# Moving statistics, bias adds and operand sums in the order of a fused decoder kernel

## The chip, the cores and the metric

The kernel runs on one core of one Trainium2 chip. The metric is the device time of one execution, in microseconds (us). All data are 32-bit floats. TensorE (PE) does the matmuls and transposes, VectorE (DVE), ScalarE (ACT) and GpSimd (POOL) the rest, and SyncE (SP) issues the DMAs.

## The reference

One pre-norm decoder layer on x of 4 sequences x 2048 positions x 512 features, in three residual parts:

```python
x = x + _L0_attn_ref(_layernorm(x), ...)    # a linear recurrence over the first axis (4 steps), in 8 blocks of 64
x = x + _L0_xattn_ref(_layernorm(x), ctx)   # cross-attention to 77 keys, 16 heads of 32
x = x + _L0_ffn_ref(_layernorm(x), ...)     # 512 -> 2048, butterfly, gelu, butterfly, 2048 -> 512
```

The layer norm subtracts the mean and divides by the root of variance + 1e-5; it has no weights. In the last part the butterflies (11 stages of 2x2 mixing) are linear, so `up butterfly` and `down butterfly` can be multiplied into the two weight matrices. Biases stand before the gelu (`hbias` in the kernel) and at the output (`b_con + down_bias`, `ybias` in the kernel).

## The kernel before, in words

**Units.** The 2048 positions are cut into 16 units of 128 positions, each with all 4 sequences: a tile `xt` of 128 x 4 x 512, which is updated in place. The work of a unit has two halves: `front` (first and second residual part, and the third norm) and `feed_forward` (third part). While `feed_forward(u)` runs, it draws the steps of `front(u+1)`, a Python generator, in between its own matmuls.

**Slots and steps.** `feed_forward` calls `step()` after every two matmul calls; one such piece is a slot. A matmul call of these shapes is two instructions on TensorE, so a slot is four. Of 108 slots (7 x 8 in the first product, then 26 x 2 in the second), the first 98 are used to draw 54 steps of the front (L762): step n is drawn at slot 98n/54, rounded up; in the first unit the first 8 slots (`lead`) are left out.

**A front,** in the order of its steps: `normed_pairs` (first norm: statistics, rows `xp`, transposes L599), four steps of the recurrence (`ps_s`, L629), `normed` (second norm: statistics, rows `xn` L561, transposes L570, copies `xnt` by ScalarE), `seven` (the query product in seven block products by Strassen's scheme, `ps_q`), attention for four t (scores `ps_sc`, exponentials by ScalarE into `pr` L679, transposes `ps_pt`, `ps_o`), the operand sums `sw` (L713 to L716), `seven` again (`ps_w`, L614, added onto `xt` in L722 and L726), and `normed` again (third norm). `combine` (L741 to L744) then makes the operand sums for the first product of the feed-forward.

**The statistics** (`norm_stats`): four L535 on VectorE, each 128 x 512, four L536, and a chain of 13 small steps on 128 x 4 elements (L541 to L548; an inverse square root by Newton's method). `normed` yields a number of steps between the statistics and the rows (2 in the second norm, 3 in the third).

**feed_forward.** The first product takes p = 0 to 7, seven block products each (L776): `up_head` (3), `up_tail` of the one before (2), `up_mid` (2), with adds on VectorE (L795, L807, L808, L816, L819) and gelu on ScalarE (L781). At each p a slice of `xt` gets the output bias on GpSimd (L844; in the first unit two larger adds, L847). The second product (L872) is made of 26 block products (`DOWN`); its left operands are sums that GpSimd makes (`made`, L829) and its right operands come from DRAM (`dn26`, L865). Results are added onto `xt` (L887, L889).

**The right operands.** The 26 right operands are 8 plain quarters of rows of the second weight matrix and 18 sums of them, in two rings of nine (`RIGHT`). `_right_sums` makes the 18 sums for one of four quarters j, `_right_stores` stores the two rings and the plain part to `dn26` (three DMAs, L151). Quarter 0 is made in the preparation, wholly on GpSimd (L140); quarters 1 to 3 are made during p = 0, 1, 2 of the first unit's feed-forward, 11 of the 18 sums on GpSimd (the names in `SLOW`) and 7 on VectorE (L142). A ring can be written again when its store has landed. The rows of quarters 1 to 3 in SBUF are later used for other things: for weights and activations (`w2` holds the weights for p = 4).

**The preparation** (`_prepare`) multiplies the butterflies into the weights. It has its own generator, and the loop at L971 draws one step of it (n = 0 to 40) and mostly one of `front(0)`.

**What sets the order.** The program is traced in Python order, and a planner then orders the instructions of each engine by their place in the program and by when it expects their inputs. In the preparation the orders of TensorE, SyncE and GpSimd are fixed by hand (L925), and for p < 4 of the first unit that of TensorE. Elsewhere an instruction may be moved ahead of others that were traced before it. `tc.keep_in_program_order(i)` pins instruction `i` behind the instruction of its engine that was traced just before it. In the kernel before it is used for the first statistics of unit 1 alone:

```python
yield from normed_pairs(xt, got, tc.keep_in_program_order if u == 1 else lambda i: i)
```

Of the kernel before, what the change touches and what calls it, by code (L numbers as in the profile page):

```python
# [14 lines left out]
ALU = mybir.AluOpType  # L15
AX = mybir.AxisListType

P = 128
T, B, D = 4, 2048, 512
# [5 lines left out]
NU = B // P  # L25
# [53 lines left out]
          ("20", "b21", "+", "b31"), ("17", "9", "+", "b31"), ("10", "14", "+", "20"), ("19", "b30", "-", "17"),  # L79
          ("22", "b01", "+", "15")))  # L80
PLAIN = tuple(f"b{k}{n}" for k in range(4) for n in range(2))
SLOW = "12", "9", "7", "18", "15", "16", "20", "17", "10", "19", "22"
SLOT = {name: i for i, name in enumerate([row[0] for lot in RIGHT for row in lot] + list(PLAIN))}
SLOT.update({str(i): SLOT[b] for i, b in ((11, "b01"), (13, "b10"), (23, "b11"), (25, "b20"), (3, "b30"), (6, "b30"),
                                          (0, "b31"), (21, "b31"))})
# [45 lines left out]
def _right_sums(nc, j, wdn, rings, alone):  # L131

    made = {f"b{k}{d}": wdn[:, 4 * j + k, d * (D // 2) : (d + 1) * (D // 2)] for k in range(4) for d in range(2)}
    for lot, ring in zip(RIGHT, rings):
        w = ring.rearrange("p (s d) -> p s d", s=len(lot))
        for i, (name, x, op, y) in enumerate(lot):
            made[name] = w[:, i, :]
            x, y, op = made[x], made[y], ALU.add if op == "+" else ALU.subtract
            if alone or name in SLOW:
                nc.gpsimd.tensor_tensor(made[name], x, y, op)  # L140
            else:
                nc.vector.tensor_tensor(made[name], x, y, op)  # L142


def _right_stores(nc, j, wdn, rings, dn26):
    lots = [ring.rearrange("p (s d) -> p s d", d=D // 2) for ring in rings]
    lots.append(wdn[:, 4 * j : 4 * j + 4, :].rearrange("p k (n d) -> p (k n) d", n=2))
    at = 0
    for w in lots:
        n = w.shape[1]  # L150
        nc.sync.dma_start(out=dn26[at : at + n, :, j, :].rearrange("s p d -> p s d"), in_=w)  # L151
        at += n


# [346 lines left out]
def kernel(ctx: ExitStack, tc: tile.TileContext, x, ctx_t, ssm_vec, ssm_vt, ssm_vinv, wq_t, wk_t, wv_t,  # L501
                        wo_t, wexp_t, up_low, up_high, up_bias, dn_low, dn_high, wcon, b_con, down_bias, out):
    nc = tc.nc
# [13 lines left out]
    ybias = const.tile([P, D], F32, name="ybias")  # L517
# [53 lines left out]
            nc.scalar.copy(xnt[:, :, t, :], ps)  # L571
        res.append(xnt)

    def normed_pairs(xt, res, keep):


        mv, y = norm_stats(xt, keep)
        xpt = work.tile([P, T // 2, D // NS, P], F32, tag="xnt", bufs=2, name="xpt")
        half = D // 2
        yield  # L580
        rows = {}

        def row(n):
            i, h = divmod(n, 2)
            rows[n] = work.tile([P, NC, 2, NS], F32, tag="xn", name="xp")
            for k in range(2):
                t = 2 * i + k
                nc.vector.tensor_scalar(rows[n][:, :, k, :], xt[:, t, h * half : (h + 1) * half].rearrange("p (f n) -> p f n", n=NS),
                                        mv[:, t, 0:1], y[:, t : t + 1], ALU.subtract, ALU.mult)

        row(0)
        for n in range(T):
            i, h = divmod(n, 2)
            if n + 1 < T:
                row(n + 1)
            yield
            ps = psum.tile([P, NC, P], F32, tag="f", name="ps_t")
            for f in range(NC):
                nc.tensor.transpose(ps[:, f, :], rows[n][:, f, :, :].rearrange("p k n -> p (k n)"), ident)  # L599
            nc.scalar.copy(xpt[:, i, NC * h : NC * h + NC, :], ps)  # L600
        res.append(xpt)
# [17 lines left out]
    def front(u, xt, res, wq=None):  # L619


        got = []
        yield from normed_pairs(xt, got, tc.keep_in_program_order if u == 1 else lambda i: i)
        xpt = got.pop()
        for c in range(NC):
            ps = psum.tile([P, T, P], F32, tag="f", name="ps_s")
# [89 lines left out]
        nc.gpsimd.tensor_tensor(s4, a12, s2, ALU.subtract)  # L716
        yield
        yield
        left = {1: a11, 2: a12, 3: s4, 4: a22, 5: s1, 6: s2, 7: s3}

        def onto(r):
# [6 lines left out]
        yield from seven((1, 6, 2, 7, 5, 4, 3), lambda i, r, k: left[i][:, k, r, :], lambda i, r, k: wo[:, i - 1, k, :], "w",  # L728
                         {1: spread, 6: onto(r12), 2: onto(r11), 7: onto(r22), 5: onto(r22), 4: onto(r21), 3: onto(r12)})

        yield from normed(xt, got, 3)
        res.append((u, xt, got.pop()))
        if u:
            combine(res[-1][2], res)

    def combine(xnt, res):

# [9 lines left out]
    def feed_forward(u, xt, rhs, other):  # L747
# [9 lines left out]
        lead = 0 if u else 8  # L757

        def step():
            slot[0] += 1  # L760
            past = slot[0] - lead
            for _ in range(max(past, 0) * 54 // (98 - lead) - max(past - 1, 0) * 54 // (98 - lead)):  # L762
                next(other, None)

        def bank(tag):
# [65 lines left out]
        for p in range(h):  # L831
            with tc.manual_schedule(engines={mybir.EngineType.PE}) if u == 0 and p < 4 else nullcontext():
                up_head(p)
                if p:
                    up_tail(p - 1)
                up_mid(p)
            if u == 0 and p < 3:
                _right_sums(nc, p + 1, wdn, rings, False)
                _right_stores(nc, p + 1, wdn, rings, dn26)
            if p == (1 if u else 6) and u + 2 < NU:  # L840
                xts[u + 2] = load_x(u + 2)
            r, d = xt[:, p // 2, p % 2 * (D // 2) : (p % 2 + 1) * (D // 2)], slice(p % 2 * (D // 2), (p % 2 + 1) * (D // 2))
            if u:
                nc.gpsimd.tensor_tensor(r, r, ybias[:, d], ALU.add)  # L844
            elif p % 2 and p > h // 2:
                r = xt[:, p - 5 : p - 3, :]
                nc.gpsimd.tensor_tensor(r, r, ybias.unsqueeze(1).to_broadcast([P, 2, D]), ALU.add)  # L847
            if p >= h // 2:
                made(*plan.pop(0)[1:])
        up_tail(h - 1)  # L850
# [6 lines left out]
        for kind, where, *rest in plan:  # L857
# [3 lines left out]
            i, name, goes = DOWN[rest[0]]  # L861
            n = rest[0] % 2
# [14 lines left out]
            while goes:  # L877
# [5 lines left out]
                d = int(to[0][2]) * (D // 2)  # L883
                r = xt[:, t : t + (k - 1) * by + 1 : by, d : d + D // 2]
# [27 lines left out]
    at, homes = 0, {}  # L912
# [5 lines left out]
    spare = {n: homes[n].rearrange("p (j q) -> p j q", q=P) for n in own}  # L918
    spare.update({n: tb[:, i].rearrange("p (j q) -> p j q", q=P) for i, n in enumerate(lent)})
    rings = [arena[:, i * 9 * D // 2 : (i + 1) * 9 * D // 2] for i in range(2)]  # L920
    xts = {}
    ready = []
    early = []
    E = mybir.EngineType
    with ExitStack() as stack, tc.manual_schedule(engines={E.PE, E.SP, E.Pool}):  # L925
# [45 lines left out]
        for n, _ in enumerate(prep):  # L971
            if n == 27:
                _right_sums(nc, 0, wdn, rings, True)
            if n not in (10, 24, 25, 26):
                next(first, None)
            if n == 3:
                quarter_loads(wo, wo_t, (0, 1, 2, 6))
                nc.gpsimd.tensor_tensor(wo[:, 4], wo[:, 6], wo[:, 0], ALU.subtract)
                nc.gpsimd.tensor_tensor(wo[:, 6], wo[:, 2], wo[:, 6], ALU.subtract)
                nc.gpsimd.tensor_tensor(wo[:, 5], wo[:, 2], wo[:, 4], ALU.subtract)  # L980
                nc.gpsimd.tensor_tensor(wo[:, 3], wo[:, 1], wo[:, 5], ALU.subtract)
            if n == 24:
                xts[1] = load_x(1)
            if n == 25:
                early.append(work.tile([P, 7, 2, P], F32, tag="qt", bufs=1, name="w_second"))
                nc.sync.dma_start(out=early[1], in_=up7[1])
            if n == 17:
                early.append(work.tile([P, 7, 2, P], F32, tag="pt", bufs=1, name="w_first"))
                nc.sync.dma_start(out=early[0], in_=up7[0])
# [19 lines left out]

    combine(ready[0][2], ready)  # L1010
    early.append(up_weights(2))
    _right_stores(nc, 0, wdn, rings, dn26)
    early.append(up_weights(3))
    for u in range(NU):
        other = front(u + 1, xts.pop(u + 1), ready) if u + 1 < NU else iter(())
# [72 lines left out]
```

## Time and profile before

| what | value |
|---|---|
| median of 3 runs | 2652.1 us (2651.93 to 2652.49) |
| the profiled execution | 2652.0 us |
| its span, first to last instruction | 2650.2 us |
| instructions | 39402 |
| preparation and front 0, before the first L776 | 193.0 us |
| from a third norm's wait to that of the next unit | 156 us |
| L535, 128 x 512 on VectorE, 192 times | 0.66 us |
| L140, 128 x 256 on GpSimd, 51 times | 0.73 us |
| L829, 128 x 512 on GpSimd, 448 times | 1.37 us (1.27 undisturbed) |
| L844, 128 x 256 on GpSimd, 120 times | 0.72 us (median) |

The page lists busy time by engine, the chain of work that ended last, and the costliest groups. A wait is idle time of an engine ahead of an instruction, put down to the instruction that released it. A window's row has its length, then busy time and (number of instructions) of TensorE, its weight loads, VectorE, ScalarE and GpSimd, then the granted clock of TensorE as a share of full speed, the share of busy DMA engines and GB/s. A row of the timeline has start, duration, engine, line, operation, operands and count.

### The profile page before, as it was taken

What the parts mean: (1) busy time and instruction counts of PE and PEld (TensorE: products, weight loads), DVE (VectorE), ACT (ScalarE), POOL (GpSimd) and SP (SyncE); (2) the same over time, 40 slices, a digit from 0 to 9 for tenths busy, and PEclk for the clock granted to TensorE, in tenths of its full rate; (3) what the DMA queues carried; (4) which work ended last, traced back from release to release, by engine and by line L of the source; (5) the groups of instructions that cost most, each with busy time, mean ns of one, the idle gap of its engine ahead of it and who ended that gap; (6) DMA issues with size and microseconds to landing.
All of it is one profiled execution on the core that took longest, in us unless ns stands there. A gap on an engine that the chain in (4) does not pass through costs nothing.

```text
span 2650.2 us, 39402 instructions
## 1 busy us (share of the span) xinstructions
PE 2530.7 (95%) x14280; PEld 2136.8 (81%) x14280; DVE 1611.8 (61%) x3489; ACT 1047.0 (40%) x3263; POOL 945.4 (36%) x842
## 2 busy tenths in 40 slices
PE   8897999999999999999999999999999999999999
PEld 5766888788888878888887888888788887878888
DVE  6666565746656575665757557575755657576553
ACT  2442615235261533626143362624436162443621
POOL 4435421514333161423315142341524225142334
PEclk9998999999999999999999999999999999999999
DMA  5738444444544444454534445443454544444446
GB/s 176 254 100 283 161 141 166 146 161 144 204 149 159 156 148 166 144 199 153 169 140 153 169 151 199 147 161 139 158 179 151 188 144 160 144 156 163 163 166 239
DMA packets 143219, 440.70 MB, mean 166 GB/s; under 512 B 20657, under 2 KB 48433, under 8 KB 140209
## 3 DMA queue, kind: packets, MB, share of 16 engines
q1 hardware_dynamic: 143026, 438.18, 48.4%
q8 instruction: 115, 1.88, 0.3%
q14 instruction: 78, 0.64, 0.1%
HBM read 398.27 MB, written 39.86 MB: 165 GB/s over the span
## 4 chain that ended last, share of the span: by engine, by line
PE 78%; DVE 19%; POOL 1%; issue 1%; DMA 1%; ACT 1%; SPq 0%; DVEq 0%; ACTq 0%; POOLq 0%
PE ps_b L776 10%; PE ps_a L872 8%; PE ps_c L776 7%; PE ps_q L614 7%; PE ps_a L776 7%; PE ps_b L872 6%; PE ps_c L872 6%; PE ps_w L614 5%; PE ps_sc L674 5%; DVE st L535 4%; PE ps_pt L694 4%; PE ps_s L629 3%; PE ps_o L704 3%; PE ps_t L570 2%; DVE xn L561 2%; DVE w L546 1%
## 5 line engine op out<-in xcount | busy, mean ns | idle before, releaser
L829 POOL TENSOR_TENSOR arena<-arena 128x512 f32<-128x512 f32 x448 | 611.3, 1372 | 1223.1 <-ACT arena L781 780.9
L781 ACT ACTIVATE arena<-arena,hbias 128x256 f32<-128x256 f32 x384 | 192.0, 508 | 400.2 <-DVE arena L816 213.6
L679 ACT ACTIVATE pr<-ps_sc,low 128x77 f32<-128x77 f32 x960 | 297.1, 331 | 49.7 <-DVE low L677 47.5
L776 PE MATMUL ps_b<-arena 128*128 128x256 f32 x1128 | 290.1, 379 | 1.5 <-DVE arena L807 1.5
L571 ACT COPY xnt<-ps_t 128x512 f32<-128x512 f32 x128 | 74.9, 586 | 545.0 <-PE ps_t L570 545.0
L776 PEld LDWEIGHTS ps_b<-arena 128*128 128x128 f32 x1128 | 208.8, 190 | 31.8 <-DVE arena L807 1.9
L872 PE MATMUL ps_a<-arena 128*128 128x256 f32 x896 | 225.9, 379 | 0.0
L679 ACT ACTIVATION_READ_ACCUMULATOR pr<-ps_sc,low 128x1 f32 x960 | 202.7, 211 | 0.0
L776 PE MATMUL ps_a<-xnt,arena 128*128 128x256 f32 x752 | 194.0, 381 | 0.1
L872 PE MATMUL ps_c<-arena 128*128 128x256 f32 x768 | 186.2, 382 | 0.0
L872 PEld LDWEIGHTS ps_a<-arena 128*128 128x128 f32 x896 | 164.5, 190 | 25.6
L677 DVE TENSOR_REDUCE low<-ps_sc 128x4 f32<-128x308 f32 x240 | 114.7, 478 | 109.5 <-PE ps_sc L674 107.2
L674 PE MATMUL ps_sc<-kbd,qt 128*128 128x308 f32 x480 | 164.6, 430 | 0.0
L872 PEld LDWEIGHTS ps_c<-arena 128*128 128x128 f32 x768 | 145.9, 193 | 19.5
L776 PEld LDWEIGHTS ps_a<-xnt,arena 128*128 128x128 f32 x752 | 141.1, 191 | 19.6 <-PE ps_b L776 0.4
L694 PE MATMUL ps_pt<-ident,pr 128*77 128x128 f32 x1024 | 149.8, 279 | 4.3 <-DVE pt L699 4.1
L614 PE MATMUL ps_q<-xnt,wq 128*128 128x256 f32 x640 | 151.2, 379 | 2.3 <-POOL xnt L659 2.3
L694 PEld LDWEIGHTS ps_pt<-ident,pr 128*77 128x77 f32 x1024 | 114.7, 147 | 43.6 <-ACT pr L679 13.4
L570 PE MATMUL ps_t<-ident,xn 128*128 128x128 f32 x512 | 84.0, 291 | 63.8 <-DVE xn L561 61.3
L872 PE MATMUL ps_b<-w,arena 128*128 128x256 f32 x512 | 143.5, 402 | 0.0
L792 ACT COPY arena<-ps_a 128x256 f32<-128x256 f32 x128 | 48.1, 376 | 230.0 <-PE ps_a L776 230.0
L570 PEld LDWEIGHTS ps_t<-ident,xn 128*128 128x128 f32 x512 | 64.3, 149 | 90.5 <-issue 57.4
(232 smaller groups left out, 5066.4 us busy)
## 6 DMA issues: line engine op xcount, KB each, us to landing
arena<-dn SPq DMA_DIRECT2D x256, 512.0 KB, 3.5
w<-dn SPq DMA_DIRECT2D x160, 512.0 KB, 3.7
arena<-up SPq DMA_DIRECT2D x79, 896.0 KB, 4.5
wq<-wq SPq DMA_DIRECT2D x16, 1792.0 KB, 8.4
w<-up SPq DMA_DIRECT2D x32, 896.0 KB, 5.6
xt<-in_x SPq DMA_DIRECT2D x11, 1024.0 KB, 5.9
dn<-arena SPq DMA_DIRECT2D x8, 1152.0 KB, 5.6
out<-xt SPq DMA_DIRECT2D x33, 256.0 KB, 2.2
```

The costliest lines, as they stand in the source:

```text
L535: keep(nc.vector.bn_stats(st[:, t, :], xt[:, t, :]))
L570: nc.tensor.transpose(ps[:, c, :], rows[t][:, c * P : (c + 1) * P], ident)
L614: nc.tensor.matmul(tiles[key][:, r, :], lhsT=lhs(i, r, k), rhs=rhs(i, r, k), start=key == i and r == 0 and k == 0, stop=k == 1, skip_group ...
L629: nc.tensor.matmul(ps[:, 2 * i : T, f * NS : (f + 1) * NS], lhsT=xpt[:, i, c * (P // NS) + f, :], rhs=gt[:, 0 : T - 2 * i, :], start=i == ...
L674: nc.tensor.matmul(ps[:, 0 : 4 * NK], lhsT=qt[:, g, t, :], rhs=kbd[:, t, g, :], start=True, stop=True)
L677: nc.vector.tensor_reduce(low, sc, AX.X, ALU.min)
L679: nc.scalar.activation(pr[:, 4 * g + h, :], sc[:, h, :], AF.Exp, bias=low[:, h : h + 1], scale=-1.0, accum_out=sm[:, 4 * g + h : 4 * g + h ...
L694: nc.tensor.transpose(pt_ps[0:NK, j, :], pr[:, 4 * g + j, :], ident)
L776: nc.tensor.matmul(ps, lhsT=w[:, c, :], rhs=rhs[i - 1][:, c], start=first and c == 0, stop=c == 1, skip_group_check=True)
L781: nc.scalar.activation(out, x, AF.Gelu, bias=hbias[:, b : b + 1])
L829: nc.gpsimd.tensor_tensor(place(p), place(x), place(y), ALU.add if op == "+" else ALU.subtract)
L872: nc.tensor.matmul(ps, lhsT=left[:, j, :], rhs=pair[:, n, j, :], start=first and j == 0, stop=j == NB // 4 - 1, skip_group_check=True)
```

## The change

1. **First statistics.** At the end of `front(u)`, behind `combine`, the statistics of the first norm of unit u+1 are traced (for u from 1 to 14), with their L535 kept in program order. `normed_pairs` takes them ready made.
2. **Output bias.** L844 and L847 are kept in program order.
3. **Two more steps.** One more `yield` behind the `sw` sums, and 4 steps in place of 3 in the third norm; `feed_forward` draws 56 steps in 98 slots. In the preparation `front(0)` also advances at n = 10 and n = 26.
4. **Operand sums.** Of the 18 sums of a quarter only four stay on VectorE in quarters 1 to 3 (`FAST`); three more than before ("4", "14", "2") go to GpSimd.
5. **Stores of quarter 0.** The plain part and the first ring are stored at n = 31 of the preparation, within SyncE's fixed order, the second ring between the loads of the weights for p = 2 and p = 3.

```diff
-SLOW = "12", "9", "7", "18", "15", "16", "20", "17", "10", "19", "22"
+FAST = "24", "5", "1", "8"
...
-            if alone or name in SLOW:
+            if alone or name not in FAST:
                 nc.gpsimd.tensor_tensor(made[name], x, y, op)
...
-def _right_stores(nc, j, wdn, rings, dn26):
+def _right_stores(nc, j, wdn, rings, dn26, which):
...
-    for w in lots:
+    for i, w in enumerate(lots):
         n = w.shape[1]
-        nc.sync.dma_start(out=dn26[at : at + n, :, j, :].rearrange("s p d -> p s d"), in_=w)
+        if i in which:
+            nc.sync.dma_start(out=dn26[at : at + n, :, j, :].rearrange("s p d -> p s d"), in_=w)
...
-    def normed_pairs(xt, res, keep):
+    def normed_pairs(xt, res, stats):
...
-        mv, y = norm_stats(xt, keep)
+        mv, y = stats
...
-        yield from normed_pairs(xt, got, tc.keep_in_program_order if u == 1 else lambda i: i)
+        yield from normed_pairs(xt, got, stats.pop(u) if u in stats else norm_stats(xt, tc.keep_in_program_order if u else lambda i: i))
...
         nc.gpsimd.tensor_tensor(s4, a12, s2, ALU.subtract)
         yield
         yield
+        yield
...
-        yield from normed(xt, got, 3)
+        yield from normed(xt, got, 4)
         res.append((u, xt, got.pop()))
         if u:
             combine(res[-1][2], res)
+        if u and u + 1 < NU:
+            stats[u + 1] = norm_stats(xts[u + 1], tc.keep_in_program_order)
...
-            for _ in range(max(past, 0) * 54 // (98 - lead) - max(past - 1, 0) * 54 // (98 - lead)):
+            for _ in range(max(past, 0) * 56 // (98 - lead) - max(past - 1, 0) * 56 // (98 - lead)):
...
-                _right_stores(nc, p + 1, wdn, rings, dn26)
+                _right_stores(nc, p + 1, wdn, rings, dn26, (0, 1, 2))
...
             if u:
-                nc.gpsimd.tensor_tensor(r, r, ybias[:, d], ALU.add)
+                tc.keep_in_program_order(nc.gpsimd.tensor_tensor(r, r, ybias[:, d], ALU.add))
             elif p % 2 and p > h // 2:
                 r = xt[:, p - 5 : p - 3, :]
-                nc.gpsimd.tensor_tensor(r, r, ybias.unsqueeze(1).to_broadcast([P, 2, D]), ALU.add)
+                tc.keep_in_program_order(nc.gpsimd.tensor_tensor(r, r, ybias.unsqueeze(1).to_broadcast([P, 2, D]), ALU.add))
...
+            if n == 31:
+                _right_stores(nc, 0, wdn, rings, dn26, (2, 0))
-            if n not in (10, 24, 25, 26):
+            if n not in (24, 25):
                 next(first, None)
...
-    _right_stores(nc, 0, wdn, rings, dn26)
+    _right_stores(nc, 0, wdn, rings, dn26, (1,))
```

More of the change, by code (lines that the diff above doesn't have):

```diff
@@ L920 @@
     rings = [arena[:, i * 9 * D // 2 : (i + 1) * 9 * D // 2] for i in range(2)]
-    xts = {}
+    xts, stats = {}, {}
     ready = []
```

## The prediction

> **What bounds the kernel now.** I read the page's totals first, then the chain that ended last, then TensorE's waits, then one unit of the steady state closely.
>
> ```profile
> PE 2530.7 (95%) x14280; PEld 2136.8 (81%) x14280; DVE 1611.8 (61%) x3489; ACT 1047.0 (40%) x3263; POOL 945.4 (36%) x842
> PE 78%; DVE 19%; POOL 1%; issue 1%; DMA 1%; ACT 1%; SPq 0%; DVEq 0%; ACTq 0%; POOLq 0%
> ```
>
> TensorE sets the time, yet VectorE holds 19% of the chain: somewhere TensorE stands still for it. TensorE's waits over the whole span (engine, line, releaser: us, times, longest):
>
> ```profile
> PE ps_t L570 <- DVE xn L561: 61.3, 32, 3.3
> PE ps_t L599 <- DVE xp L588: 12.0, 3, 9.1
> PE ps_w L614 <- DVE sw L714: 7.7, 15, 0.5
> ...
> PE ps_b L776 <- DVE arena L795: 6.6, 1, 6.6
> ```
>
> The first row is the transposes of a norm waiting for its first normed row. By start times 13 of these waits are 3.3 us, one in each front of units 2 to 14, at the third norm; 14 more are 0.78 us, at the second norm of the fronts of units 2 to 15. The third row is 0.5 us in each front. What VectorE does before the long wait, in the unit that stands at 658 us:
>
> ```profile
> 660.33 1.85 DVE L535 BATCH_NORM_STATS2 st<-xt 128x6 f32<-128x512 f32 x3
> ...
> 662.63 0.66 DVE L535 BATCH_NORM_STATS2 st<-xt 128x6 f32<-128x512 f32 x1
> 663.21 1.21 DVE L541 TENSOR_SCALAR v<-mv 128x4 f32<-128x4 f32 x1
> ...
> 665.77 0.66 DVE L535 BATCH_NORM_STATS2 st<-xt 128x6 f32<-128x512 f32 x1
> ...
> 668.35 0.66 DVE L535 BATCH_NORM_STATS2 st<-xt 128x6 f32<-128x512 f32 x1
> ...
> 670.26 0.24 DVE L546 TENSOR_TENSOR w<-y,v 128x4 f32<-128x4 f32 x2
> 670.46 0.24 DVE L547 TENSOR_TENSOR w<-w,y 128x4 f32<-128x4 f32 x2
> ```
>
> A norm needs four of L535. Here eight run: four are the next unit's first statistics, which the planner has put in among the third norm's, and its small steps follow in pairs (x2). The small steps should take 0.16 us; L541 takes 1.21 because a GpSimd sum (L829, 1.27 us) runs over it.
>
> The last front, of unit 15, has no next unit. That is an experiment in the same trace: the stretch from the second group of ps_w matmuls (L614) to the next feed-forward's first matmul (L776), and the windows after the waits (columns: us, busy time by engine, then granted TensorE clock):
>
> ```profile
> 648.12:687.10 38.98, 35.66 (x165) 30.85 (x166) 30.89 (x73) 2.34 (x4) 19.24 (x18) 0.96 0.45 148
> 2518.74:2553.78 35.04, 33.97 (x164) 29.59 (x165) 23.80 (x48) 2.34 (x4) 19.09 (x18) 1.00 0.50 162
> ...
> 671.50:676.00 4.50, 4.46 (x17) 3.80 (x18) 4.34 (x8) 1.17 (x2) 4.50 (x6) 0.62 0.09 36
> ...
> 2539.00:2543.00 4.00, 3.95 (x23) 3.57 (x24) 3.00 (x7) 1.17 (x2) 4.00 (x5) 1.00 0.72 249
> ```
>
> Without the foreign statistics VectorE is busy 23.8 us in place of 30.9, the stretch is 3.94 us shorter, and the wait is 1.07 us in place of 3.32. After 3.32 us of idleness the clock falls to 0.62 for 4.5 us; after 1.07 us it stays at 1.00.
>
> **What the skill says.** "TensorE: Matmul & The Clock Gate", section "What's actually happening": an idle window of about 3.4 us drops the clock to half, and it takes such a window to recover. The trace agrees: 3.32 us of idleness does it. The work from 671.54 to 675.86 (4.32 us) takes 2.62 us after the last front's wait, so a long wait costs 1.70 more than its length. "SBUF — State Buffer", section "Who interferes with whom": some VectorE forms and GpSimd share a pair of ports under an exclusive lock held for a whole instruction. The trace agrees for small steps (1.21 against 0.16 us) and shows none for L535 (0.66 us with or without a sum beside it).
>
> **The change, part by part.**
>
> *First statistics of the next unit in line.* They are now traced behind combine, each L535 pinned behind the VectorE instruction traced before it; the first hangs behind combine's L743, which needs the transposed third norm, so they cannot run ahead of it. This removes from the third norm's chain 4 x 0.58 us (0.66 less the overlap with the neighbour) = 2.3, 4 aggregates of 0.09 net, and the next unit's small steps. By the last front, 2.25 us of wait and 1.70 us of slow clock go: 3.94 us. Where they go: at 658 us L743 ends at 681.8; statistics (2.6 us), two additions of products (L887, L889, 1.1 us) and a chain of 13 small steps (1.3 us free, up to 5.8 more if all eight bias adds of 0.72 us hold them) give 686.8 to 692.6, and the first xp rows 0.8 later. TensorE wants them at 692.3; VectorE stood idle there for 1.3 to 2.2 us at a time. I take no wait; the far end is 2.5 us, since on VectorE no row can stand behind more than L808 (692.5; the next of its kind needs matmuls that are queued behind the transposes), after which 1.5 us of small steps and 0.8 us of rows follow.
>
> *Two more front steps.* The 54 steps that fill 98 slots become 56. By the step's formula (step n falls on slot 98n/54, now 98n/56, rounded up) the third norm's transposes come 10 slots after the last ps_w group, not 9 as in the last front; a slot is 4 matmul instructions of 0.216 us = 0.86 us. The last front's 1.07 us falls to 0.2 (2.25 + 1.70 + 0.87 = 4.8 us a unit). The extra step behind the sw sums is 7 slots, not 6, and 0.86 covers the 0.52 us wait: 0.5 a unit. Price: every other step gets 1.75 slots, not 1.81. Attention's first part starts at slot 44 instead of 46 and its 12 steps span 21 slots, not 22; the last unit of probabilities is ready about 1.8 us before its transposes, so 0.86 less still covers.
>
> *Output bias in line.* L844 ran as soon as the xn rows were written (671.5 to 678.0) and made L546 to L548 of the next unit 0.65 us each. Now the adds come after combine, five at once and three among the down sums. Their number is the same; nobody waits before the down products. I cost it at nothing; if it holds rows it is inside the 2.5 us above.
>
> *First unit, GpSimd sums and stores.* Here TensorE loses 6.6 us (behind VectorE sums of L142 that wait 5.2 us for stores), 9.1 (rows of unit 1), 1.5 and 2.5 us (195 to 370 us), with some 6 us of slow clock. Per quarter three of seven L142 sums go to GpSimd (9 x 0.73 = 6.6 us more there), the two bias adds of 2.4 us go later, and two stores of the first quarter are issued before combine. VectorE no longer waits for the second ring's stores. But SyncE must still issue three quarters of stores before the weights for p=4 (issued 235.5, landed 246.1), and TensorE used these at 246.8: what is gained earlier is waited for there, unless the stores move. A ring's cycle is its sums (9 x 0.73) and a store (5.6), 12.2 us; the second quarter's second ring can start at 202 and is summed at 208.6, and two cycles later the last store goes out, at 233 against 234.3. In SyncE's queue the two stores now precede the load of b for the hidden bias (L494), which was at 174.6 and goes to 188.8; L496 and the first gelu (196.7) stand behind it. A load of b landed in 3.0 us once and in 12.1 us behind other loads. The third store now follows the weights for p=2, which so leave some 3 us before 195.6; they are used at 212.5, so this is worth nothing. Front 0's two more steps fall on two turns of the preparation (10 and 26) in which it stood still; its own waits there are under 0.8 us each, and I count no change. So the part is worth between -3 (a late b) and 12 (all stalls up to 224 us); I take 4: the 2.5 us wait and its slow clock, which the pause at p=4 hides.
>
> **The sum.** 13 units x (4.8 + 0.5) = 69. Unit 1's front: waits 0.85 + 2.07 at the third norm, 0.5 and 0.9 of slow clock = 4.3, take 4. Unit 15: 0.9 + 0.5 = 1.4. First unit: 4. Together 78.6. The profiled execution took 2652.0 us (span 2650.2 and 1.8 around it), the median is 2652.1: 2652.0 - 78.6 = 2573.
>
> **Rivals.**
> 1. *The wait is replaced.* A GpSimd sum holds two more small steps of the third norm (2 x 1.27), or the first norm gets the 2.5 us worked out above. Under 3.3 us the clock holds, so a unit gains 2.8 less: 2573 + 13 x 2.5 = 2606. For it: in the last front three steps were still held, for 1.2, 0.8 and 1.1 us. Against: TensorE arrives 0.86 us later than there. 0.15.
> 2. *More goes.* The second norm's 0.78 us comes because its second row meets the first GpSimd sum (row 716.60, sum 716.43); with front steps a slot earlier the row passes first: 14 x 0.78 = 11. With 8 us more of the first unit: 2554. 0.14.
> 3. *Slower, by ScalarE.* Gelu and exponential change tables, 2 x 1.28 us a pair, 5 pairs a unit. Attention now overlaps 12 slots of the up phase, not 10. Three more pairs (7.7 us) less the cover of 0.9 would be 6.8 us a unit, over the 5.3 gained from the point where the loss passes 5.3: 2652 + 13 x 1.5 - 9 = 2663. Against: the extra slots hold one gelu group, so one pair. 0.04.
> 4. *It doesn't do what it says.* Excluded for the statistics by the dependency on combine; 0.01 for a null result.
>
> **How the numbers follow.** The forecast case has 0.66, its own range 2556 to 2591 (a 1.2 us remainder in 13 units is 16, the first unit's ends -8 and 7, part of the second norm's 11). With rivals 1 and 2 the 8-in-10 range is 2550 to 2600. Faster or slower counts from 0.2% (5.3 us), about what a measurement here tells from no change. Faster 0.95, same 0.01, slower 0.04.
>
> **What would show it.** Right: no 3 us wait of L570 for L561 after 370 us and no clock below 1.00 there; four L535 between the last L722 and the row, four behind L743; L844 behind L744; no wait of ps_w for L714. The first-unit step: the waits for L795 and L588 shrink, but one at p=4 appears. Wrong: waits at L599, at pr (ScalarE), or a unit period above 152 us (now 156).

## The result, and the profile after

| | before | after |
|---|---|---|
| median of the runs, us | 2652.0 (4 runs) | 2633.1 (4 runs, 2629.1 to 2636.8) |
| ratio, 95% interval | | 0.9929 [0.9912, 0.9946] |
| profiled execution / its span, us | 2652.0 / 2650.2 | 2632.0 / 2630.2 |
| mean period of a unit (units 3 to 12), us | 155.93 | 153.77 |
| start of the first up phase, us | 193.03 | 197.01 |
| first unit, from there to the next up phase, us | 181.36 | 184.64 |

The change gains 19 us where 79 were forecast. A unit's period here is the time from its first up matmul (of the first product; L776 before, L780 after) to that of the next unit, from the trace. The products of the second half are called down products. Most lines of the changed kernel stand 1 to 4 further down: the third norm's transposes are now L571, the rows L562, the down products L876, GpSimd's down sums L833.

The totals and the chain of the page after:

```profile
PE 2526.9 (96%) x14280; PEld 2126.0 (81%) x14280; DVE 1599.6 (61%) x3480; ACT 1039.9 (40%) x3263; POOL 935.2 (36%) x851
PE 76%; DVE 14%; ACT 7%; issue 1%; DMA 1%; POOL 1%; SPq 0%; DVEq 0%; ACTq 0%; POOLq 0%
```

VectorE's share of the chain fell from 19 to 14%, and ScalarE's rose from 1 to 7%. TensorE's waits after say what holds it now:

```profile
PE ps_a L876 <- DVE xt L893: 15.7, 9, 1.8
PE ps_t L571 <- DVE xn L562: 13.7, 17, 7.2
...
PE ps_a L876 <- DVE arena L893: 8.7, 5, 1.8
...
PE ps_w L615 <- DVE sw L715: 7.8, 15, 0.5
PE ps_a L876 <- ACT arena L785: 5.8, 14, 0.4
PE ps_b L780 <- issue: 5.4, 14, 0.4
```

The 3.3 us waits at the transposes are gone, and so are the 0.78 us at the second norm. But 14 waits of 1.74 us are new, at a down product that needs a PSUM bank (a piece of the memory that TensorE writes to) which L893 has yet to empty; two new waits of 0.4 us a unit stand at the ends of the up phase, and the wait of ps_w for sw has not moved. The third norm in the unit that stands at 662 us, all engines in order of time:

```profile
664.21 7.89 POOL L833 TENSOR_TENSOR arena<-arena 128x512 f32<-128x512 f32 x6 [10.78 <-PE ps_b L876]
...
666.29 0.57 DVE L542 TENSOR_SCALAR v<-mv 128x4 f32<-128x4 f32 x1
...
667.10 1.12 DVE L544 TENSOR_SCALAR y<-vi 128x4 int32<-128x4 int32 x1
668.13 0.16 DVE L545 TENSOR_SCALAR v<-v 128x4 f32<-128x4 f32 x1
668.32 1.11 DVE L547 TENSOR_TENSOR w<-y,v 128x4 f32<-128x4 f32 x1
...
671.01 1.11 DVE L548 TENSOR_TENSOR w<-w,y 128x4 f32<-128x4 f32 x1
672.05 0.67 DVE L893 TENSOR_TENSOR arena<-arena,ps_a 128x512 f32<-128x512 f32 x1
...
672.78 1.13 PE L876 MATMUL ps_a<-w,arena 128*128 128x256 f32 x4 [1.74 <-DVE arena L893]
...
673.42 0.55 DVE L562 TENSOR_SCALAR xn<-xt,mv,y 128x512 f32<-128x512 f32 x1
...
674.11 0.63 PE L571 MATMUL ps_t<-ident,xn 128*128 128x128 f32 x4 [0.20 <-DVE xn L562]
```

Only the norm's own statistics are left here, as the change meant. Yet six GpSimd sums run back to back from 664.21 to 672.1, and five of the thirteen small steps take 0.6 to 1.1 us in place of 0.16: one step slips through between two sums, the next is held until its sum ends. Behind nine of these steps VectorE's queue has L893, the eviction: it adds the product in the bank to a tile in SBUF, and so frees the bank for TensorE's next product. From the first small step to the row it is 7.1 us.

### The profile page after: what moved, and what is told of

Same layout as the page of the kernel before. It is cut to its first block, busy times and chain, and to the rows that moved or that the text cites. A ratio compares the mean times of both kernels' runs of the same rounds, so it can differ in the third digit from the quotient of the medians.

```text
span 2630.2 us, 39485 instructions
## 1 busy us (share of the span) xinstructions
PE 2526.9 (96%) x14280; PEld 2126.0 (81%) x14280; DVE 1599.6 (61%) x3480; ACT 1039.9 (40%) x3263; POOL 935.2 (36%) x851
## 4 chain that ended last, share of the span: by engine, by line
PE 76%; DVE 14%; ACT 7%; issue 1%; DMA 1%; POOL 1%; SPq 0%; DVEq 0%; ACTq 0%; POOLq 0%
PE ps_b L780 11%; PE ps_a L876 9%; PE ps_a L780 7%; PE ps_q L615 7%; PE ps_c L780 7%; PE ps_c L876 6%; PE ps_w L615 5%; PE ps_b L876 4%; PE ps_pt L695 3%; PE ps_sc L675 3%; ACT pr L680 3%; PE ps_s L630 3%; PE ps_o L705 3%; PE ps_t L571 2%; DVE st L536 2%; ACT L785 1%
## 5 line engine op out<-in xcount | busy, mean ns | idle before, releaser
L833 POOL TENSOR_TENSOR arena<-arena 128x512 f32<-128x512 f32 x448 | 601.2, 1348 | 1288.8 <-ACT arena L785 780.8
L780 PE MATMUL ps_b<-arena 128*128 128x256 f32 x1128 | 293.2, 380 | 8.7 <-issue 5.4
L780 PEld LDWEIGHTS ps_b<-arena 128*128 128x128 f32 x1128 | 207.6, 190 | 40.8 <-issue 10.6
L876 PE MATMUL ps_a<-arena 128*128 128x256 f32 x896 | 223.2, 379 | 0.0
L780 PE MATMUL ps_a<-xnt,arena 128*128 128x256 f32 x752 | 196.4, 380 | 1.3 <-ACT arena L785 1.3
L876 PEld LDWEIGHTS ps_a<-arena 128*128 128x128 f32 x896 | 165.7, 190 | 26.4
L876 PE MATMUL ps_c<-arena 128*128 128x256 f32 x768 | 184.4, 380 | 0.2
L876 PE MATMUL ps_a<-w,arena 128*128 128x256 f32 x512 | 133.8, 385 | 30.1 <-DVE xt L893 15.7
L876 PEld LDWEIGHTS ps_c<-arena 128*128 128x128 f32 x768 | 144.0, 190 | 22.8 <-DMA arena<-dn 2.5
L780 PEld LDWEIGHTS ps_a<-xnt,arena 128*128 128x128 f32 x752 | 143.3, 191 | 23.6 <-ACT arena L785 1.6
L820 DVE TENSOR_TENSOR arena<-ps_b,arena 128x256 f32<-128x256 f32 x128 | 54.0, 422 | 137.1 <-PE ps_b L780 137.1
L615 PEld LDWEIGHTS ps_q<-xnt,wq 128*128 128x128 f32 x640 | 121.4, 190 | 19.1 <-POOL xnt L660 2.6
```

The costliest lines, as they stand in the source:

```text
L615: nc.tensor.matmul(tiles[key][:, r, :], lhsT=lhs(i, r, k), rhs=rhs(i, r, k), start=key == i and r == 0 and k == 0, stop=k == 1, skip_group ...
L780: nc.tensor.matmul(ps, lhsT=w[:, c, :], rhs=rhs[i - 1][:, c], start=first and c == 0, stop=c == 1, skip_group_check=True)
L833: nc.gpsimd.tensor_tensor(place(p), place(x), place(y), ALU.add if op == "+" else ALU.subtract)
L876: nc.tensor.matmul(ps, lhsT=left[:, j, :], rhs=pair[:, n, j, :], start=first and j == 0, stop=j == NB // 4 - 1, skip_group_check=True)
```

## The experiments

**Theory A**: what is left of the third norm's wait is the small steps held by GpSimd's sums. **Theory B**: the two added front steps cost time. Rivals: the order of VectorE's queue alone; the pins; the first unit's part; the clock. Where the change adds or removes parts, the kernels below do one part alone or undo one.

| kernel | median us | ratio to before, 95% | unit, us |
|---|---|---|---|
| p_stats: statistics in line alone | 2610.9 | 0.9842 [0.9827, 0.9856] | 152.95 |
| p_steps: two steps alone | 2661.3 | 1.0032 [1.0020, 1.0044] | 156.75 |
| a_oldfirst: after, first unit's part undone | 2629.5 | 0.9910 [0.9893, 0.9928] | 154.39 |
| a_nopin: after, no bias pins | 2629.9 | 0.9909 [0.9895, 0.9923] | 154.26 |
| a_free0: after, first unit's bias adds free | 2631.8 | 0.9911 [0.9896, 0.9926] | 154.67 |
| a_nosteps: after, two steps undone | 2614.7 | 0.9863 [0.9847, 0.9880] | 153.01 |
| a_quarter: after, thin down sums | 2584.3 | 0.9745 [0.9730, 0.9759] | 151.12 |
| a_ahead5: after, sums 5 ahead | 2597.6 | 0.9794 [0.9780, 0.9809] | 151.61 |
| s_ahead5: p_stats, sums 5 ahead | 2592.5 | 0.9773 [0.9759, 0.9788] | 151.67 |
| s_ahead3: p_stats, sums 3 ahead | 2595.2 | 0.9780 [0.9767, 0.9792] | 151.67 |
| a_pin3: after, eviction first | 2674.1 | 1.0077 [1.0065, 1.0088] | 157.02 |
| s5_norm: s_ahead5, a step in the third norm | 2598.3 | 0.9795 [0.9781, 0.9809] | 152.18 |
| s5_mid: s_ahead5, a step at ps_w | 2599.8 | 0.9800 [0.9786, 0.9814] | 152.18 |
| s5_first: s_ahead5, first unit's part | 2593.0 | 0.9777 [0.9763, 0.9791] | 151.67 |
| s5_later: s_ahead5, up-phase sums later | 2592.4 | 0.9772 [0.9760, 0.9785] | 151.65 |
| s5_thin: s_ahead5, first such sum thin | 2595.6 | 0.9776 [0.9763, 0.9790] | 151.67 |
| s5_keep: s_ahead5, such sums behind L644 | 2576.0 | 0.9721 [0.9707, 0.9734] | 150.71 |

### The parts alone

p_stats is the kernel before with the edits of normed_pairs, front and `stats` of the diff; p_steps the one with its third yield, `normed(xt, got, 4)` and 56.

> The kernel before with one part alone: the next unit's first statistics traced behind combine. The first unit's part, the pins of the bias adds and the two steps stay as they were. Theory A (small steps held by GpSimd's down sums are what is left of the third norm's wait): the row comes when it comes in the changed kernel, TensorE one slot (0.86 us) earlier, so about 2.8 us of waiting a unit in place of 3.3, no slow clock behind it: 156.3 - 0.5 - 1.7 = 154.1 us a unit, about 2620 us in all. If the place in line did nothing by itself and the steps did it: 2645 to 2652.

> The kernel before with one part alone: two more front steps (56 in place of 54). Theory A: the third norm's chain of eight statistics and its held small steps is as long as before, TensorE arrives one slot later: the wait falls from 3.3 to about 2.5 us, and [...]1.7 us more go: 153.8 us a unit, about 2617 us. The two parts would then replace each other more than they add up. If the steps cost elsewhere what they cover: 2645 to 2652.

The statistics alone gain 41 us, more than twice what the whole change does; the steps alone lose 9. Waits of p_stats, then of p_steps:

```profile
PE ps_t L570 <- DVE xn L561: 29.5, 31, 2.1
```

```profile
PE ps_t L570 <- DVE xn L561: 53.5, 18, 3.7
...
PE ps_a L873 <- ACT arena L782: 5.8, 14, 0.4
```

In p_stats the third norm's wait is 1.07 us in every steady unit, as in the last front of before. In p_steps it grew to 3.7, and the clock fell at 12 of these 13 waits. TensorE's queue says why one slot more did not help. Behind the last ps_w group stand 42 down instructions in p_steps and 40 in before; but between the ps_w groups stand 6 in p_steps and 8 in before, so from the last matmul of the attention (ps_o) to the transposes there are 48 in both. A wait for gelu (0.41 us) at the start of the down phase is new. With p_stats the planner left 44, 36 of them behind the last group: it also goes by when it expects the row. p_stats is 9 us better than I expected since I took after's late row for it: with this queue three small steps are held (1.18, 0.83 and 1.12 us), not five. Its sums run in two lots, with a pause:

```profile
655.43 3.97 POOL L831 TENSOR_TENSOR arena<-arena 128x512 f32<-128x512 f32 x3 [8.62 <-PE ps_b L874]
660.61 3.97 POOL L831 TENSOR_TENSOR arena<-arena 128x512 f32<-128x512 f32 x3 [1.21 <-PE ps_a L874]
```

The last front of p_steps has no next statistics, so there the steps stand alone. It looks like every front of after: six sums without a pause, five held steps, and a wait at the product for the bank (L890 is the eviction):

```profile
PE ps_a L873 <- DVE arena L890: 1.8, 1, 1.8
```

### After, less one part

```
a_nosteps:  - third yield at sw; normed(xt, got, 3); 54 for 56
a_oldfirst: SLOW list, stores together, pauses 10 and 26 back, L851 without keep_in_program_order
a_nopin:    L848 and L851 without keep_in_program_order
a_free0:    L851 alone without it
```

> The changed kernel with the two front steps taken back (54 steps); statistics in line, bias pins and the first unit's part stay. Theory B (the two steps are what costs: they put a product whose PSUM bank VectorE has not yet emptied ahead of the transposes, and new waits at the start of the down phase): units of 152.9 us as with the statistics alone, 2611 to 2617 us depending on what the first unit's part and its pinned adds cost. If the steps are harmless and pins or first unit cost the rest: about 2630.

> The changed kernel with its first unit's part undone: the old share of the first unit's operand sums on VectorE, the old place of the stores, the old two pauses of the preparation, and the first unit's bias adds free again. If that part costs time (late stores and weights, two bias adds of 2.4 us over a norm's small steps): 7 to 12 us less than the changed kernel, 2621 to 2626. If the first 381 us are longer for another reason (the TensorE clock at 140 us): 2632 to 2634.

> The changed kernel with no bias add kept in line, in all units. If the pins are nearly inert in units 1 to 15 and in unit 0 a pinned add of 2.3 us holds a small step of the second norm: about 3 us less, 2630. If the pins are what holds small steps in every unit: 0.7 us a unit or more, 2622 or less.

> The changed kernel with only the first unit's two bias adds (2.3 us each) free again. If these, kept in line, hold the second norm's small steps of front 1 (the 7.2 us wait of the transposes at 255 us): 3 to 5 us less than the changed kernel, 2628 to 2630. If they do not matter: 2633.

Theory B holds: without the two steps the changed kernel takes 2614.7, so on top of the rest they cost 18.5 us. The two profiled executions, 18.3 us apart, say where: 10 us in the units from the second on (0.6 in most of them), 5.3 in the first unit, and 3.0 before the first up phase, where TensorE's clock fell in the execution of after only (below). The last 3.0 cannot be laid to the steps. The other three differ from after by 1 to 4 us, less than their intervals tell apart. The trace of a_free0 shows the pin's harm all the same: in after a bias add of 2.34 us (L851, 249.29) holds a small step of front 1's second norm for 2.26, and the transposes wait 7.15 us at 255 us; in a_free0 they wait 2.04. The first unit is 5.3 us shorter there (179.35 in place of 184.64). It is not the pin alone: a_nosteps keeps the pin, has a wait of 7.8 us there, and its first unit takes 179.34. So these 5.3 us and those of the steps above are the same; taking back either one regains them. The medians of after and a_free0 do not tell the gain apart: steady units of a_free0 took 153.6 to 156.2 us.

### The sums

```
a_quarter: made(): place(p)[:, 0:1], place(x)[:, 0:1], place(y)[:, 0:1]
ahead5:    _down_plan(5, 4, own, lent, 17)     ahead3: _down_plan(3, 4, own, lent, 17)
a_pin3:    third norm: yield three times between the aggregates and L542; keep_in_program_order(L542)
```

The first argument of `_down_plan` says how many products ahead of its use a sum is planned; it was 4.

> The changed kernel with GpSimd's down sums made over a quarter of their width (128 of 512 elements; the rest of each sum is left out, so the outputs are not the reference's). Each engine's order of instructions is that of the changed kernel. Theory A (GpSimd's sums hold the small steps of the third norm): a sum takes about 0.4 us, a held step no longer than that; the wait of the product for the bank (1.74 us) and of the transposes for the row (0.21) go, 151.7 us a unit, about 2606 us. If only the order on VectorE (the eviction behind nine small steps) makes the wait: 2628 to 2633.

> The kernel before with the statistics in line alone, and GpSimd's down sums planned five products ahead in place of four: the same sums, some 0.9 us or more earlier, VectorE's and TensorE's orders the same. Theory A: one or two small steps fewer are held (1.1 us each), the third norm's wait of 1.07 us a unit goes: 2596 to 2600 us. If the sums do not matter: 2611.

> The changed kernel with GpSimd's down sums planned five products ahead in place of four, each engine's order the same. Theory A: one or two small steps fewer are held ahead of the eviction, its wait falls from 1.74 us by 1.1 or all: 2610 to 2618 us. If the sums do not matter: 2633.

> The kernel before with the statistics in line alone, GpSimd's down sums planned three products ahead in place of four: the same sums, one product (0.9 us or more) later; VectorE's and TensorE's orders the same. Theory A: one small step more is held, or the held ones lie later, the third norm's wait grows from 1.07 by 0.9 to 1.1 us a unit: 2623 to 2627 us. If the gain of five ahead came from something else than the meeting with the small steps: 2611 or less.

> The changed kernel with the small steps of the third norm kept behind the eviction that empties the bank (traced three steps later, the first one kept in line); TensorE's order is the same. If VectorE's order makes the wait: the 1.74 us go and nothing comes back, about 2608 us. Theory A (the sums hold the small steps): the eviction is early, the chain of small steps starts later and still meets the sums, the row comes no earlier, and the wait moves from the product to the transposes: 2628 to 2636 us.

In all five the order of TensorE's instructions is that of the kernel compared with, and so is VectorE's, but for a_pin3's edit. GpSimd's own order changes in each; in a_quarter the short sums also run earlier. Thin sums take away 2.65 us a unit, more than theory A asked: 2584. What the rest comes from was not traced further. With the sums five products ahead, the third norm's wait is gone in both families. Sums and small steps of s_ahead5, all engines in time:

```profile
650.52 3.98 POOL L831 TENSOR_TENSOR arena<-arena 128x512 f32<-128x512 f32 x3 [8.62 <-PE ps_b L874]
...
654.73 0.17 DVE L541 TENSOR_SCALAR v<-mv 128x4 f32<-128x4 f32 x1
...
657.47 0.17 DVE L548 SCALAR_TENSOR_TENSOR y<-w,y 128x4 f32<-128x4 f32 x1
657.67 0.55 DVE L561 TENSOR_SCALAR xn<-xt,mv,y 128x512 f32<-128x512 f32 x1
```

The last sum ends at 654.50, the chain starts at 654.73 and takes 2.9 us with L891 in the midst of it: all steps are free. s_ahead3 fell out against my expectation. I took the sums to come one product later and hold one step more; instead the wait for a free space left one sum beside the chain and moved four past the first row:

```profile
658.62 1.26 POOL L831 TENSOR_TENSOR arena<-arena 128x512 f32<-128x512 f32 x1 [13.80 <-PE ps_a L874]
...
658.72 1.18 DVE L548 SCALAR_TENSOR_TENSOR y<-w,y 128x4 f32<-128x4 f32 x1
...
661.59 0.55 DVE L561 TENSOR_SCALAR xn<-xt,mv,y 128x512 f32<-128x512 f32 x1
```

One sum, one held step, no wait. The number expected was wrong, the mechanism is confirmed from the other side: five held steps go with 1.95 us of waits (after), three with 1.07 (p_stats), two (a_ahead5), one or none with no wait at all. In a_pin3 VectorE's order is put right and the time gets worse (its lines stand 2 to 25 further down: L918 is the eviction, L901 the product, L596 the transposes):

```profile
667.40 0.69 DVE L918 TENSOR_TENSOR arena<-arena,ps_a 128x512 f32<-128x512 f32 x1 [1.25 <-PE ps_a L901]
668.01 1.19 DVE L544 TENSOR_SCALAR v<-mv 128x4 f32<-128x4 f32 x1
...
671.93 1.18 DVE L550 TENSOR_TENSOR w<-w,y 128x4 f32<-128x4 f32 x1
...
674.73 1.00 DVE L587 TENSOR_SCALAR xn<-xt,mv,y 128x512 f32<-128x512 f32 x2
...
675.42 0.63 PE L596 MATMUL ps_t<-ident,xn 128*128 128x128 f32 x4 [3.74 <-DVE xn L587]
```

The product no longer waits, but the eviction first waits 1.25 us for its own product, the chain starts 1.9 us later (counted from the last ps_o matmul), meets the sums all the same, and the whole wait stands at the transposes. At 3.74 us the clock falls, in all 14 such fronts. The Trainium skill, "TensorE: Matmul & The Clock Gate", "What's actually happening", puts the idle window that lowers it at some 3.4 us, and this trace agrees (shorter waits stand at the end of this text): in the windows of this kernel (us, busy by engine, clock) TensorE is at 0.62 behind the wait.

```profile
675.50:680.00 4.50, 4.50 (x18) 3.62 (x19) 1.59 (x5) 0.65 (x2) 3.08 (x4) 0.62 0.25 89
```

I had put it at 2628 to 2636: the direction was right, the size missed the second chain of delay and the clock. The order of VectorE's queue is not the cause; it only chose where TensorE waited.

### A step as a slot, and the first unit's part

s5_norm and s5_mid add one yield (55 for 54), in the third norm or behind the first group of `seven` for ps_w; s5_first adds the diff's FAST list, stores and pauses.

> The kernel before with statistics in line, the sums five products ahead, and one front step more, in the third norm (55 steps). With the row no longer late, one more slot of cover ahead of the transposes has nothing left to hide: the rest of the third norm's wait (some 0.2 us a unit) may go, new waits at the start of the down phase may come: 2588 to 2595 us. If a slot is worth 0.86 us a unit as the formula of the steps says: 2580.

> As the kernel with statistics in line and sums five products ahead, with one front step more, put right between the first group of ps_w products and the group that needs the sw sums (55 steps). If a step is a slot in TensorE's queue: the wait of ps_w for sw (0.5 us in each front) goes, 0.5 us a unit. If TensorE's queue is filled by the planner and not by the steps: two down instructions stand between the two groups as before, the wait stays at 0.5 us, 2588 to 2595 us.

> As the kernel with statistics in line and sums five products ahead, with the first unit's part added (more operand sums on GpSimd, two stores of the first quarter early, the two pauses of the preparation dropped), but the first unit's bias adds free. If that part is worth its 4 us: 2588. If the late load of b and the later weights take back what the sums give: 2592 or a few us more.

s5_mid puts its yield exactly between the two ps_w groups. TensorE's queue there is unchanged (four down instructions between them, as in before) and the wait stays:

```profile
PE ps_w L614 <- DVE sw L716: 7.8, 15, 0.5
```

In s5_norm the yield did move the transposes by the slot that the formula gives: 40 down instructions behind the last ps_w group in place of 36. But the four that stood between the last two groups are gone, so from the attention on there are 44 in s_ahead5, s5_norm and s5_mid. Wherever the extra step is put, a unit is 0.5 us longer; spread over 14 units that is the 6 to 7 us. TensorE's waits in a unit are no longer than in s_ahead5, so where this half microsecond comes from stays open. s5_first is level with s_ahead5: the first unit's part is worth nothing that can be measured.

### The second norm

> As the kernel with statistics in line and sums five products ahead, with the first of the four sums made in the up phase moved from the fifth to the sixth turn (the next ones follow a turn later, two in the last). If this sum holds the second normed row of the second norm (1.49 in place of 0.55 us): the 0.78 us wait goes, 14 x 0.78 = 11, about 2581 us. If the wait is another's: 2592.

> As the kernel with statistics in line and sums five products ahead, but the first GpSimd sum of the up phase of units 1 to 15 is made over a quarter of its width (128 of 512 elements; the rest of this sum is left out, so the outputs are not the reference's). All queues keep their order. If this sum holds the second normed row of the second norm: the row takes some 0.6 to 0.7 us and the wait of 0.78 us goes or falls to 0.1, 14 x 0.7 = 10 us, about 2582. If the wait is another's: 2592.

> As the kernel with statistics in line and sums five products ahead, with the four GpSimd sums of the up phase traced in its seventh and eighth turns and kept in line, which puts them behind the GpSimd difference after the second norm (L644); all sums are made in full. If a sum that meets the second normed row makes the second norm's wait: the row takes 0.55 us, the 0.78 us go in 14 fronts, 2592.5 - 11 = 2581.5 us. If the wait is another's: 2592.

All three keep the orders of TensorE and VectorE of s_ahead5. The first two did not test it. In s5_later the sum moved in the program, but it waits for a gelu (L783) and ran at the same moment beside the row; in s5_thin the short sum needed less and ran 18 us earlier, and the next one took its place. s5_keep puts the sums behind L644. Rows and sum of s_ahead5, then the rows of s5_keep:

```profile
855.74 1.96 DVE L561 TENSOR_SCALAR xn<-arena,mv,y 128x512 f32<-128x512 f32 x2
856.03 1.38 POOL L831 TENSOR_TENSOR arena<-arena 128x512 f32<-128x512 f32 x1 [33.76 <-ACT arena L783]
```

```profile
848.97 1.00 DVE L561 TENSOR_SCALAR xn<-arena,mv,y 128x512 f32<-128x512 f32 x2
```

The two rows take 1.00 us in place of 1.96, the wait is gone, and a unit is 0.96 us shorter, the first unit 3.6: 2576.0 us, with 5 us more than expected. This is the fastest kernel of the study, 0.9721 [0.9707, 0.9734] of before.

## Why the prediction was wrong

The parts, each measured on top of the ones above it (2652.0 to 2633.1), beside what the forecast's sum gave them:

| part | forecast | measured |
|---|---|---|
| statistics in line (13 x 3.95, and 4.3 in unit 1) | -56 | -41 (p_stats) |
| pins and first unit's part | -4 | +4 (a_nosteps less p_stats; their intervals overlap) |
| two front steps (13 x 1.37, and 1.4 in unit 15) | -19 | +18 (after less a_nosteps) |

- **Two more front steps** is the step that failed, with 37 of the 60 us missed. Each unit was to gain 0.87 us at the third norm and 0.5 at ps_w; it lost 0.6 to 0.7. The slots were counted rightly, and priced wrongly. Behind the last ps_w group there are 9 slots with the statistics alone and 10 in after, as the formula says, and at the transposes 0.2 us of the 1.07 is left, as forecast. Three things were put at nothing:
  - The count began at the last ps_w group, and that group moved too: ahead of it stand two down instructions where there were four. Counted from the last ps_o matmul, 46 down instructions come before the transposes, 44 with the statistics alone. That is 0.43 us of cover, not 0.86.
  - GpSimd's sums moved as well. The product that frees a space for the first of them stands behind the last ps_w group in after (ps_b at 663.11), ahead of it in p_stats. Counted from the start of the last ps_o matmul (648.65 in after, 642.02 in p_stats) the sums start at 15.6 us in place of 13.4, and they run without the pause. They hold five steps and not three, and the row starts at 24.8 us in place of 23.2: 1.6 later, for 0.43 of cover.
  - The product in the tenth slot itself needs VectorE, whose eviction stands behind nine small steps. So the wait is 1.74 us there and 0.20 at the transposes.

The down products of after behind its last ps_w group, 40 instructions with the four of the product that waits, shown above:

```profile
663.11 1.03 PE L876 MATMUL ps_b<-w,arena 128*128 128x256 f32 x4
663.97 1.89 PE L876 MATMUL ps_c<-arena 128*128 128x256 f32 x8
665.70 3.62 PE L876 MATMUL ps_a<-arena 128*128 128x256 f32 x16
669.15 1.89 PE L876 MATMUL ps_c<-arena 128*128 128x256 f32 x8
```

- "0.86 covers the 0.52 us wait" failed in another way: the yield behind the sw sums moved nothing. No down instruction stands between the last ps_o and the first ps_w group, and four between that and the group that needs sw, in before and in after. Nor did s5_mid's yield in that very place add one. The price list named only less cover (0.86 us), and not the 0.41 us at the first down product. The sw wait may well be of theory A's kind: in before L714 takes 1.64 us beside GpSimd's L715 (1.77 us), while L713 of the same size takes 0.69. No run here tested it.
- **Rival 1 came**, two more held steps, by another road than it was given: it was priced as a loss of 2.5 us a unit from the 0.2 expected, and after shows 1.95 us of waits. "Against: TensorE arrives 0.86 us later than there" was the count above: from the attention on it arrives 0.43 us later, and the row 1.6.
- **Statistics in line**: right in place and mechanism. The four L536 (L535 before) run behind L747, and L600 waits for them in no steady unit. 3.94 us a unit from the last front was too much by about 1: a new wait of 0.3 us stands at a product of the first up turn (0.45 us from start to start), because VectorE empties its bank (L797 in p_stats, which ends 0.1 us before the product starts) behind four xp rows; and in four of the thirteen units of before the clock had not fallen at all (155.0 to 155.3 in place of 156.3 us), though TensorE waited as long. The forecast charged the 1.70 us to all thirteen. The last front was a good experiment for the wait, which in p_stats is 1.07 as there.
- **Output bias in line**: "now the adds come after combine, five at once" was wrong. The pin is to the last GpSimd instruction traced before, and four of eight L848 still ran right behind the rows (674.04). In steady units it cost nothing that shows; in the first unit the pinned L851 and the two steps together cost 5.3 us (traces of a_free0 and a_nosteps).
- **First unit**: the sign was wrong in the trace (+3.3 us there), the value nothing by s5_first. The load of b landed at 202.5 us and held hbias, as the far end feared. Of the preparation's +4.0 us some 3 are not the change's: TensorE's clock in the window 137 to 146 us was 0.62 in this execution and 1.00 in that of before. a_nosteps, a_nopin and a_free0 have after's preparation without that fall and start the first up phase at 194.0 to 194.5 us; s_ahead5 and s5_thin both have before's and start at 193.0 and 197.9, with clocks of 1.00 and 0.62.
- **Second norm** (rival 2): its mechanism is now shown (s5_keep). In after the gain came as described, the rows pass before the sum (872.06 and 872.48); it was paid for elsewhere by the steps.
- **ScalarE** (rival 3): there are as many table loads as before (76 for gelu and 76 for the exponentials), and in a steady unit only the 0.41 us wait is new. Its 7% of the chain comes with that wait: p_steps has both, p_stats neither.

What stays open: why single units of the changed kernel and its near variants take 154 to 155 in place of 153.6 us, where those of s_ahead5, s_ahead3, a_ahead5 and s5_keep repeat to 0.2 us from the third on (the three units of 156 us in a_free0 each hold one fall of the clock, shown below); where the 0.5 us of a single added step comes from; and why TensorE's clock falls at 137 us in some executions.

## What to carry to other kernels

When a planner fills the queues, a changed step moves more than the place it was meant for. Compare the queues of all engines before pricing it in slots, count from a point that did not move (here the last ps_o), and price a filler by what the filler itself waits for. The chain of thirteen tiny dependent VectorE steps took from 2.9 to 7.1 us here, by how many GpSimd sums ran beside it. So first look whether that work can run a few microseconds earlier or later: here that was one constant, worth 18 us on p_stats and 36 on after, where the whole change gave 19. And test parts alone: two parts that each look like cover for the same wait can undo each other.

## What the runs showed of the hardware

- Held steps alternate with the sums: of the small steps of 0.16 us in after, every second one took 0.57 to 1.12 us as long as sums of 1.27 us ran, waiting for one to end. This is as the Trainium skill, "SBUF — State Buffer", "Who interferes with whom", has it: a lock held for a whole instruction. With 128 elements in place of 512 a sum took about 0.5 us. A chain took 2.9 us free (s_ahead5), 3.9 with one held step, 5.6 with three, 7.1 with five. A normed row (128x512) beside a sum took 1.49 in place of 0.55 us, while L536 stayed at 0.65 to 0.70.
- The length of one wait does not say whether TensorE's clock falls. Behind a wait of 3.32 us it fell in nine fronts of before and stayed at 1.00 in four; behind 3.72 it fell in 12 of 13 (p_steps), behind 3.75 in 14 of 14 (a_pin3). Behind 1.74 and 0.20 us close together it stayed in all 14 fronts of after, and fell in three of a_free0, to 0.50. So the 3.4 us quoted above is no threshold here. A window of before behind a wait of 3.32 us, then one of a_free0 behind 1.75 and 0.20 us:

```profile
984.50:989.00 4.50, 4.50 (x27) 3.75 (x25) 4.34 (x8) 1.76 (x3) 4.17 (x6) 1.00 0.25 66
```

```profile
1284.10:1287.50 3.40, 3.21 (x10) 2.79 (x11) 2.38 (x6) 0.59 (x1) 3.28 (x5) 0.50 0.20 80
```

- It can also fall with no long wait near: in the window 137 to 146 us of after TensorE was busy for 8.75 of 9.00 us at a clock of 0.62, and no wait in the nine microseconds ahead was over 0.78 us. In before, with waits of the same length there, it was busy for 7.72 at 1.00, for more instructions. By the starts of the first up phase 3 to 4 us are lost (194.0 in a_nosteps, 197.0 in after). The windows of after, then of before:

```profile
137.00:146.00 9.00, 8.75 (x61) 7.17 (x62) 4.82 (x7) 3.94 (x24) 3.90 (x3) 0.62 0.00 1
```

```profile
137.00:146.00 9.00, 7.72 (x73) 6.34 (x68) 5.96 (x12) 5.91 (x34) 1.25 (x1) 1.00 0.00 1
```
